# Image outputs of the last four heads computed on GpSimd, and their channels transposed once per pair

## The chip, the core and the metric

The kernel runs on one core of a Trainium2 chip. The core has five engines that work side by side, each through its own instructions in order: TensorE (PE in the profile, its weight loads PEld), VectorE (DVE), ScalarE (ACT), GpSimd (POOL) and SyncE (SP, which here only issues DMA transfers). They meet through semaphores. The metric is the device time of one execution in microseconds.

## What is computed

Two cross-attention layers run one behind the other over 64 batches of 256 tokens with 320 channels, in 20 heads of 16 channels. Each batch has 77 context rows of 512 numbers. Layer 0 is an attention over the 77 rows with a residual. Layer 1 splits its context into 73 text rows and 4 image rows, and the change lies in its image part:

```python
scores_t = jnp.einsum('bhsd,bhtd->bhst', q, k_t) * attn_scale
probs_t = jax.nn.softmax(scores_t, axis=-1)
text_out = jnp.einsum('bhst,bhtd->bhsd', probs_t, v_t)
...
attn_scores = jnp.einsum('bhsd,bhnd->bhsn', q, k_ip) * attn_scale
qsem = _l2norm(jnp.einsum('bhst,bte->bhse', probs_t, text_ehs))
sem = jnp.einsum('bhse,bne->bhsn', qsem, _l2norm(ip_ehs))
fused = attn_scores + SEM_SCALE * sem
probs_ip = jax.nn.softmax(fused, axis=-1) * spatial_mask[None, None, :, None]
ip_out = jnp.einsum('bhsn,bhnd->bhsd', probs_ip, v_ip)
...
out = (text_out + IP_SCALE * ip_out) @ W_out + b_out + residual
```

So for every token and head there are four image weights (`probs_ip`), and the image output is a weighted sum of four value rows.

## The kernel before

**Tiling.** All numbers are float32. Batches go in pairs `p` (32 of them), `b` is the batch within the pair. The 320 channels are held as two tiles of 128 (heads 0 to 15, "main") and one of 64 (heads 16 to 19, "last"). The last channels of both batches share one tile of 128 partitions: rows 0 to 63 are batch 0, rows 64 to 127 batch 1, and its 256 columns are tokens. `H` is 20, `HT` 16, `NIP` 4, `P` 128, `HALF` 64, `S` 256 tokens, in halves `s` of 128.

**Steps.** A unit is eight heads of 128 tokens, and a pair has ten. The main loop runs over steps `g`; step `k = g % 10` of pair `p = g // 10` does one unit of layer 0 and one of layer 1, which is 13 steps behind. Each step has a fixed body on TensorE: the semantic products of layer 1 (`semantics`, L755 and L761), the scores of both layers (`scores`, L641), then `transposed(1)` and `transposed(0)` (L705 and L706), which bring the softmax results into [key, token]. VectorE takes the maximum of the scores (L659), subtracts it (L661), and multiplies and sums (L772, L775, L687, L1136). ScalarE does the exponentials (L669, L672, L673) and the copies out of PSUM: L712 and L713 for `transposed(1)`, L731 and L732 (L720 and L723 for the last heads) for `transposed(0)`, and L1064 for the sums of the semantic products. L1064 frees the PSUM tile `sc` that the next step's L755 writes: there is one. GpSimd normalizes the weights of layer 0 (L692), whose result `transposed(0)` of the next step reads, and copies the image scores (`att`, L676).

**Fillers.** All other work is placed by hand into the steps by `fillers(k, p)`, in four lists: `begin` runs after the scores, `first` between `transposed(1)` and `transposed(0)`, `second` and `third` behind them, with the attention products of layer 0 (`attend`, L788 and L793, in the steps whose unit closes a block) between the two. TensorE, ScalarE, VectorE and GpSimd keep the order in which the program was written (`keep_order`); SyncE's transfers are ordered by the scheduler once the first steps are over.

**PSUM.** Eight banks: four for `sc`, two for the pool `pms` (matrix products) and two for the pool `ptr` (tag "tr", all transposes). Each call of `transposed` takes both buffers of `ptr`, first the one of L705, then the one of L706.

**The image path of a pair.** It runs two pairs behind, so `fillers` calls it with `p - 2`:

- `image_values` (steps 7 and 8, L475): per batch, 20 DMAs on SyncE, one per head, each bringing the batch's four image value rows from `vip_rows` in DRAM into the tile `vip` [80 rows (head, image row), 320 channels]; `place_image_values` (step 9, L480) masks it on GpSimd to a block diagonal.
- `text_output` (in the steps in which layer 1 finishes a batch: step 9 for batch 0, step 4 for batch 1): `by_head` (L850) divides the text sums into `an` [token, half, head, channel] on GpSimd. `text_transposed` (list `third` of steps 0 and 5) turns it into [channel, token]: per token half, two transposes for the main channels (L837) and one for the last channels (L838), into one `ptr` tile, and two copies by ScalarE (L840 main, L841 last).
- `image_scores`, `image_shifted`, `image_exponential`, `image_weights` make the four weights per token and head, in the steps after; `image_weights` writes the tile `iw` through `by_head`, in step 2 for batch 0 and step 7 for batch 1.
- `image_transposed` (step 7, list `second`): four transposes of `iw` (L914, K 128, 80 rows out) into one `ptr` tile and one ScalarE copy to `iwT` (L916).
- `image_attend` (step 8, list `begin`): the products of `vip` and `iwT` for the main channels (L926), copied by ScalarE (L936) and added to the text part by GpSimd (L938).
- `image_attend_last` (step 8, at the end of `second`): the products for the last channels (L947, two products of K 80, one per batch, side by side in the array; each is two instructions in the profile), added to the text part on VectorE (L951).
- `project` (begun in step 9, L528; its end at the start of the next step 0, L537) and `project_last` (L616) read the result.

**Neighbours of these on GpSimd.** `place_values(1, p - 1, 1)` in step 7 (L424 and L430 into `gv`, L438 and L444 into `gr`) reads the tiles `vm` and `v_rest` that SyncE fetches (L395); L755 reads `gv`, L761 reads `gr`, for batch 1 first in the next step 0. `place_gram` (L511, L515) and `keys_by_head` (L365, reading `kl`) are in step 8; `gram` (L499 to L502, and eight loads L506 into `g_rest`) in steps 0 and 6. SyncE also loads the context tile `ct` (L154), `cf` (L179) and `x` (L167, L169).

Of the kernel before, what the change touches and what calls it, by code (L numbers as in the profile page):

```python
# [8 lines left out]
F32 = mybir.dt.float32  # L9
# [54 lines left out]
def tile_two_cross_attentions(ctx: ExitStack, tc: tile.TileContext, a: dict, out: bass.AP):  # L64
# [179 lines left out]
    head_mask = blocks("head_mask", P, 8, D)  # L244
    for n in (4, 2):
        nc.gpsimd.tensor_add(head_mask[:, :n], head_mask[:, :n], head_mask[:, n : 2 * n])
    ip_mask = blocks("ip_mask", H * NIP, H, NIP)

# [218 lines left out]

    def image_values(p, b):  # L470

        n, r0 = H * NIP, (2 * p + b) * NIP
        vip = vips[p, b] = big.tile([n, C], F32, tag="vip", name=f"vip{p}_{b}", bufs=3)
        for h in range(H):
            nc.sync.dma_start(vip[h * NIP : (h + 1) * NIP, :], vip_rows[r0 : r0 + NIP, :])  # L475

    def place_image_values(p, b):
        n, vip = H * NIP, vips[p, b]
        v = vip.rearrange("p (h d) -> p h d", d=D)
        nc.gpsimd.tensor_tensor(v, v, ip_mask[:n].unsqueeze(2).broadcast_to([n, H, D]), ALU.mult)  # L480

    grams = {}

# [330 lines left out]
            nc.scalar.copy(last, ps[:, 1, :])  # L814


    def text_output(p, b):

        sums = stats[p, b][1]
        rec = small.tile([P, 2 * H], F32, tag="rec", name=f"rec{p}_{b}", bufs=2)  # L820
        nc.vector.reciprocal(rec, sums[:, :, NIP + D])
        an = big.tile([P, 2, H, D], F32, tag="an", name=f"an{p}_{b}", bufs=1)
        by_head(an, sums[:, :, NIP : NIP + D], rec)
        return an

    def text_transposed(p, b):

        an = made["an"]
        if b == 0:
            aTs[1, p] = channels("aT1", f"aT1_{p}", 1)  # L830
        main, last = aTs[1, p]
        rows = slice(b * HALF, (b + 1) * HALF)
        for s in range(2):
            ps = ptr.tile([P, 4, P], F32, tag="tr", name=f"atr{p}_{b}{s}")
            t = an[:, s].rearrange("p h d -> p (h d)")
            for i in range(2):
                nc.tensor.transpose(ps[:, i, :], t[:, i * P : (i + 1) * P], ident)  # L837
            nc.tensor.transpose(ps[: rows.stop, 2, :], t[:, C - rows.stop :], ident)  # L838
            t0 = b * S + s * P
            nc.scalar.copy(main[:, :, t0 : t0 + P], ps[:, :2])  # L840
            nc.scalar.copy(last[rows, s * P : (s + 1) * P], ps[rows, 2, :])  # L841

    one = const.tile([P, 1], F32, tag="one", name="one")

    def by_head(to, t, factor):

        n = t.shape[2]
        for s, h0, at in ((0, 0, 0), (1, HT, H), (1, 0, H + 4)):
            m = H if s == 0 else H - HT if h0 else HT
            nc.gpsimd.tensor_tensor(  # L850
                to[:, s, h0 : h0 + m], t[:, at : at + m],
                factor[:, at : at + m].unsqueeze(2).broadcast_to([P, m, n]), ALU.mult,
            )


    nums = {}
# [38 lines left out]
    def image_weights(p, b):  # L895

        num = nums[p, b]
        m = small.tile([P, 2, H], F32, tag="imx", name=f"imx{p}_{b}", bufs=1)
        r = m.rearrange("p s h -> p (s h)")
        nc.vector.tensor_reduce(r, num, AX.X, ALU.add)  # L900
        nc.vector.reciprocal(r, r)
        nc.gpsimd.tensor_mul(m, m, smask.unsqueeze(2).broadcast_to([P, 2, H]))
        to = weights[p, b] = small.tile([P, 2, H, NIP], F32, tag="iw", name=f"iw{p}_{b}", bufs=2)
        by_head(to, num, r)

    weights = {}

    def image_transposed(p):
        n = H * NIP
        ps = ptr.tile([P, 4, P], F32, tag="tr", name=f"itr{p}")  # L910
        for b in range(2):
            w = weights[p, b].rearrange("p s h t -> p s (h t)")
            for s in range(2):
                nc.tensor.transpose(ps[:n, 2 * b + s, :], w[:, s], ident)  # L914
        wT = big.tile([n, S2], F32, tag="iwT", name=f"iwT{p}", bufs=1)
        nc.scalar.copy(wT, ps[:n].rearrange("p j t -> p (j t)"))  # L916
        return wT
# [22 lines left out]
        t = big.tile([P, 2, S2], F32, tag="ip_out", name=f"ip_out{p}", bufs=1)  # L940
        return [lambda i=i: out_of(i) for i in range(2)]

    def image_attend_last(p):
        wT, last = made["wT"], aTs[1, p][1]
        ps = pms.tile([P, 512], F32, tag="ms", name=f"ipv{p}_2")
        for b in range(2):
            nc.tensor.matmul(  # L947
                ps[b * HALF : (b + 1) * HALF, :S], vips[p, b][:, 2 * P :], wT[:, b * S : (b + 1) * S],
                start=True, stop=True,
            )  # L950
        nc.vector.tensor_add(last, ps[:, :S], last)  # L951


    made = {}

    def fillers(k, p):
# [19 lines left out]
        elif k == 1:  # L976
# [3 lines left out]
                add(1, p, place_values, 0, p, 0)  # L980
            add(0, p, queries, 0, p, 2)
            add(1, p - 1, project, 0, p - 1)
            add(1, p - 1, place_gram, 0)
            add(1, p, keys_by_head, 0, p, 1)
            add(1, p - 1, keys_by_head, 1, p - 1, 0)
# [17 lines left out]
        elif k == 4:  # L1003
            if p == 0:
                add(0, p, image_keys, 1)
            else:
                add(0, p, keys, 1, p, 0)
            add(1, p - 1, values, 1, p - 1, 1)
            add(1, p + 1, first_queries, p + 1)
        elif k == 5:  # L1010
            if p == 0:
                add(0, p, image_keys, 2)
            add(0, p + 1, keys, 0, p + 1, 0)
            add(2, p - 2, text_transposed, p - 2, 1)
        elif k == 6:
            while len(made_rows) * P < min(NB, 2 * (p + 2)) * T:
                rows_todo.extend((len(made_rows), l) for l in range(2))
                made_rows.append(rows_todo[-1])
            for n in range(len(rows_todo) // 2):
                add(0, p, value_rows, *rows_todo.pop(0))  # L1020
            if p == 0:
                add(0, p, image_norms)
            else:
                add(1, p, keys, 1, p, 1)
            add(1, p - 1, gram, p - 1, 1)
            add(1, p, place_image_keys, p)
        elif k == 7:
            add(0, p + 1, keys, 0, p + 1, 1)
            add(1, p + 1, last_keys, p + 1)
            add(1, p - 2, lambda: made.update(wT=image_transposed(p - 2)))  # L1030
            add(1, p - 1, place_values, 1, p - 1, 1)
            add(1, p - 1, image_values, p - 1, 0)
            if p == 0:
                add(1, p, image_rows)
        elif k == 8:
            while rows_todo:
                add(0, p, value_rows, *rows_todo.pop(0))
            add(1, p - 1, place_gram, 1)
            add(1, p + 1, keys_by_head, 0, p + 1, 0)
            add(1, p - 1, image_values, p - 1, 1)  # L1040
            add(1, p - 2, image_attend_last, p - 2)
            add(3, p - 2, lambda: held.update(i=lambda: image_attend(p - 2)))
        else:
            add(0, p - 2, project, 1, p - 2)
            add(1, p + 1, values, 0, p + 1, 0)
            for b in range(2):
                add(1, p - 1, place_image_values, p - 1, b)
# [159 lines left out]
```

## Time and profile before

| what | value |
|---|---|
| median of 3 runs | 2614.46 us (2613.04 to 2614.5) |
| profiled execution, its own time | 2612.19 us |
| span of that profile | 2610.4 us |
| granted TensorE clock | 0.998 |
| L947 products, 128 instructions, busy together | 20.9 us |
| L838 transposes, 128 | 272 ns each in the records |
| L951 sums on VectorE, 32 | 415 ns each (median) |
| L841 copies on ScalarE, 128 | 262 ns each (median) |
| L480 masks on GpSimd, 64 | 727 ns each (median) |
| DMA share of the span, mean of 16 engines (SyncE's queue q1) | 18.0% |

In these rows a line is a line of the kernel, followed by the engine, the operation and the tiles (out<-in); "x" counts instructions. The records of TensorE overlap, since products are pipelined: a record of 0.27 us may cost 0.11 us when another follows. The chain of waits is better for that: it follows the end of the program back, and gives each piece only the time in which nothing else was the reason. An idle time in brackets stands before the instruction that ends it, with what released it. Times of day are in us from the start of the span; a pair takes 77.4 us in the steady part, or some more where a step has additional rows to project.

### The profile page before, as it was taken

Reading aid. Unit: us, or ns where it says so; the run is one execution under the profiler, and the core shown is the slowest. Engines: PE = TensorE matmul, PEld = TensorE weight load, DVE = VectorE, ACT = ScalarE, POOL = GpSimd, SP = SyncE. Lnnn points to the kernel's source line nnn. Section 1 sums busy time; section 2 is a strip of 40 time slices with the busy share of each in tenths; the row PEclk is TensorE's granted clock in tenths of the full one; section 3 lists DMA queues with packets and bytes.
Section 4 is the critical chain, followed back from the end, with each engine's and each line's share of the span. In section 5 each row is a group of like instructions: output and inputs, shape, how many; then the busy total and the mean of one; then the engine's idle time right before and its main releaser. Section 6 shows DMA issues by size and latency. Waiting matters only on the chain.

```text
span 2610.4 us, 74097 instructions
## 1 busy us (share of the span) xinstructions
PE 2552.0 (98%) x27026; PEld 1979.1 (76%) x27026; DVE 1971.3 (76%) x3641; ACT 1535.6 (59%) x3989; POOL 1439.9 (55%) x3514
## 2 busy tenths in 40 slices
PE   7999999999999999999999999999999999999998
PEld 5677777777777777777777777777777777777677
DVE  4577777777787777787777787777777778777864
ACT  3465665665665665665665665665665566666553
POOL 2456555566555556555556555556555565555542
PEclk9999999999999999999999999999999999999999
DMA  5212211112111112111112111112111112111100
GB/s 164 72 29 58 58 43 48 43 51 55 52 51 38 51 51 55 55 48 39 51 52 55 51 52 43 47 52 56 52 51 39 51 53 55 47 50 34 29 22 23
DMA packets 154658, 132.28 MB, mean 51 GB/s; under 512 B 48248, under 2 KB 132984, under 8 KB 154296
## 3 DMA queue, kind: packets, MB, share of 16 engines
q1 hardware_dynamic: 153432, 126.38, 18.0%
q8 instruction: 217, 3.56, 0.6%
q14 instruction: 145, 1.19, 0.2%
q10 hardware_dynamic: 864, 1.15, 0.1%
HBM read 89.53 MB, written 33.91 MB: 47 GB/s over the span
## 4 chain that ended last, share of the span: by engine, by line
PE 84%; DVE 7%; DMA 3%; ACT 2%; POOL 1%; issue 1%; SPq 1%; DVEq 0%; POOLq 0%; ACTq 0%
PE sc L755 12%; PE tr L705 11%; PE o_ps L528 8%; PE sc L641 7%; PE v_ps L379 6%; PE sc L761 4%; PE q_ps L528 4%; PE q_ps L555 4%; PE k_ps L334 3%; PE o_ps L616 3%; DVE w L661 3%; PE pv L788 2%; PE o_ps L537 2%; DVE mx L659 2%; PE q_ps L557 2%; PE rtr L706 2%
## 5 line engine op out<-in xcount | busy, mean ns | idle before, releaser
L659 DVE TENSOR_REDUCE mx<-sc 128x8 f32<-128x584 f32 (+1 forms) x640 | 497.3, 777 | 446.9 <-PE sc L641 446.8
L692 POOL TENSOR_TENSOR parts<-w,sm 128x512 f32<-128x512 f32 (+1 forms) x640 | 439.5, 707 | 301.9 <-ACT parts L673 177.8
L661 DVE TENSOR_TENSOR w<-sc,mx 128x616 f32<-128x616 f32 x640 | 511.8, 800 | 67.0 <-ACT w L669 0.5
L712 ACT COPY pt<-tr 128x512 f32<-128x512 f32 x320 | 186.8, 584 | 431.9 <-PE tr L705 427.5
L705 PE MATMUL tr<-ident,parts 128*128 128x128 f32 x2560 | 409.6, 283 | 12.5 <-POOL parts L692 5.2
L755 PEld LDWEIGHTS sc<-gv,pt 64*128 64x128 f32 x5120 | 316.9, 187 | 96.0 <-ACT sums L1064 47.3
L705 PEld LDWEIGHTS tr<-ident,parts 128*128 128x128 f32 x2560 | 282.5, 141 | 123.4 <-issue 88.0
L755 PE MATMUL sc<-gv,pt 64*128 64x94 f32 x5120 | 356.3, 278 | 17.4 <-ACT sums L1064 17.2
L676 POOL COPY att<-w 128x32 f32<-128x32 f32 x320 | 66.8, 209 | 469.7 <-DVE w L661 469.2
L669 ACT ACTIVATE w<-w 128x616 f32<-128x616 f32 x320 | 232.0, 725 | 96.7 <-DVE w L661 95.8
L687 DVE TENSOR_REDUCE sm<-w 128x8 f32<-128x616 f32 x320 | 247.9, 775 | 13.6 <-ACT w L669 13.6
L641 PE MATMUL sc<-kbd,q 32*128 32x154 f32 x5120 | 248.2, 306 | 1.0 <-ACT q L586 0.8
L528 PE MATMUL o_ps<-aT,wo 128*128 128x256 f32 x1024 | 231.6, 379 | 0.0
L1136 DVE TENSOR_REDUCE nrm<-prod 128x8 f32<-128x584 f32 x320 | 227.3, 710 | 0.4
L772 DVE TENSOR_TENSOR prod<-sc,parts 128x512 f32<-128x512 f32 x320 | 217.8, 681 | 4.0 <-PE sc L761 4.0
L528 PEld LDWEIGHTS o_ps<-aT,wo 128*128 128x128 f32 x1024 | 189.7, 190 | 23.0
L672 ACT ACTIVATE parts<-w 128x512 f32<-128x512 f32 x320 | 207.1, 647 | 0.0
L641 PEld LDWEIGHTS sc<-kbd,q 32*128 32x128 f32 x5120 | 187.0, 187 | 6.2 <-issue 5.4
L731 ACT COPY pt<-tr 128x512 f32<-128x512 f32 x256 | 151.1, 590 | 67.1 <-PE tr L705 66.8
L379 PE MATMUL v_ps<-wv,cf 128*128 128x320 f32 (+1 forms) x624 | 182.1, 438 | 0.0
L706 PE MATMUL rtr<-ident,parts 128*104 128x128 f32 (+1 forms) x640 | 174.8, 273 | 0.0
L1064 ACT COPY sums<-sc 128x168 f32<-128x168 f32 x320 | 96.4, 301 | 122.5 <-DVE prod L775 121.3
(151 smaller groups left out, 4840.0 us busy)
## 6 DMA issues: line engine op xcount, KB each, us to landing
vip<-vip_rows SPq DMA_DIRECT2D x1280, 5.0 KB
out_dram<-x SPq DMA_DIRECT2D x64, 256.0 KB
x<-in_x_dram SPq DMA_DIRECT2D x31, 512.0 KB
v_rows<-vs SPq DMA_DIRECT2D x38, 320.0 KB
vm<-v_rows SPq DMA_DIRECT2D x152, 80.0 KB
ct<-in_ctx_dram SPq DMA_DIRECT2D x32, 308.0 KB
cf<-in_ctx_dram SPq DMA_DIRECT2D x38, 256.0 KB
g_rest<-gram_rest SPq DMA_DIRECT2D x512, 0.5 KB
```

Source lines behind the costliest of these rows:

```text
L379: nc.tensor.matmul(ps[:n, :C], cfs[i][:, k, :n], wv[l][:, k, :], start=(k == 0), stop=(k == KE - 1))
L528: nc.tensor.matmul(ps[b][:, m, :], w[:, k, m * P : (m + 1) * P], main[:, k, b * S : (b + 1) * S], start=(k == 0 and m == 0), stop=False,)
L641: nc.tensor.matmul(ps[:, r, 2 * T * l : 2 * T * (l + 1)], q[rows, b, :] if part == 2 else q[rows, t0 : t0 + P], kbd[rows, part].rearrange( ...
L659: nc.vector.tensor_reduce(mx, sc[:, :, :, :nt], AX.X, ALU.max)
L661: nc.vector.tensor_tensor(w, sc, mx.unsqueeze(3).broadcast_to([P, 4, 2, T]), ALU.subtract)
L669: nc.scalar.activation(w, w, AF.Exp, scale=SCALE)
L687: nc.vector.tensor_reduce(sm, w, AX.X, ALU.add)
L692: nc.gpsimd.tensor_tensor(two[:, 8 * t0 : 8 * t1].rearrange("p (h t) -> p h t", h=8), w[:, :, t0:t1], sm.unsqueeze(2).broadcast_to([P, 8, ...
L705: nc.tensor.transpose(ps[:, i, :], flat[:, i * P : (i + 1) * P], ident)
L706: nc.tensor.transpose(pr[:n, 0, :], flat[:, 4 * P : 4 * P + n], ident)
L755: nc.tensor.matmul(ps[:, i % 2 * 2 + j, at : at + GV], pt[half_rows, i, :], gv[b][half_rows, part, i, :], start=start and i < 2, stop=False,)
L1136: nc.vector.tensor_reduce(eight(stats[q, b][2], u), prod, AX.X, ALU.add)
```

## The change

The four last heads leave the image path by TensorE. `iw`, `vip` and the mask shrink to 16 heads (64 rows, 256 channels, 16 DMAs per batch), and `image_attend_last` goes with its products and its sum. Instead:

- `by_head` writes the last heads (both token halves in one instruction) into a tile of their own: `lasts[p]` [token, half, batch, head, channel] for the text part, `iw_last` for the weights. It still has three instructions per call.
- `last_image_values` (steps 1 and 5) loads the batch's four value rows of 64 channels to all 128 partitions with one DMA that repeats its source (tile `vlast`, one buffer).
- `last_image_outputs` (steps 4 and 7) makes the image output as [token, head] on GpSimd: for each of the four image rows one product of [128, 2 x 4 x 16] (value row times weight) and one sum into `lasts[p]`.
- `last_transposed` (step 8, end of `second`) transposes `lasts[p]` for both batches at once: two transposes into one `ptr` tile, one ScalarE copy of 128x256 into the last channels.
- `text_transposed` keeps only the main channels.
- `place_values(1, p - 1, 1)` moves from step 7 to step 8, behind `keys_by_head`.

```diff
@@ -244,7 +244,7 @@
...
-    ip_mask = blocks("ip_mask", H * NIP, H, NIP)
+    ip_mask = blocks("ip_mask", HT * NIP, HT, NIP)
...
@@ -469,15 +469,22 @@
...
-        n, r0 = H * NIP, (2 * p + b) * NIP
-        vip = vips[p, b] = big.tile([n, C], F32, tag="vip", name=f"vip{p}_{b}", bufs=3)
-        for h in range(H):
-            nc.sync.dma_start(vip[h * NIP : (h + 1) * NIP, :], vip_rows[r0 : r0 + NIP, :])
+
+        n, r0 = HT * NIP, (2 * p + b) * NIP
+        vip = vips[p, b] = big.tile([n, 2 * P], F32, tag="vip", name=f"vip{p}_{b}", bufs=3)
+        for h in range(HT):
+            nc.sync.dma_start(vip[h * NIP : (h + 1) * NIP, :], vip_rows[r0 : r0 + NIP, : 2 * P])
 
     def place_image_values(p, b):
-        n, vip = H * NIP, vips[p, b]
+        n, vip = HT * NIP, vips[p, b]
         v = vip.rearrange("p (h d) -> p h d", d=D)
-        nc.gpsimd.tensor_tensor(v, v, ip_mask[:n].unsqueeze(2).broadcast_to([n, H, D]), ALU.mult)
+        nc.gpsimd.tensor_tensor(v, v, ip_mask[:n].unsqueeze(2).broadcast_to([n, HT, D]), ALU.mult)
+
+    def last_image_values(p, b):
+
+        r0 = (2 * p + b) * NIP
+        v = vips[p, b, "last"] = small.tile([P, NIP, HALF], F32, tag="vlast", name=f"vlast{p}_{b}", bufs=1)
+        nc.sync.dma_start(v, vip_rows[r0 : r0 + NIP, 2 * P :].unsqueeze(0).broadcast_to([P, NIP, HALF]))
...
@@ -814,13 +821,17 @@
...
+    lasts = {}
+
     def text_output(p, b):
 
         sums = stats[p, b][1]
         rec = small.tile([P, 2 * H], F32, tag="rec", name=f"rec{p}_{b}", bufs=2)
         nc.vector.reciprocal(rec, sums[:, :, NIP + D])
-        an = big.tile([P, 2, H, D], F32, tag="an", name=f"an{p}_{b}", bufs=1)
-        by_head(an, sums[:, :, NIP : NIP + D], rec)
+        an = big.tile([P, 2, HT, D], F32, tag="an", name=f"an{p}_{b}", bufs=1)
+        if b == 0:
+            lasts[p] = big.tile([P, 2, 2, H - HT, D], F32, tag="an_last", name=f"an_last{p}", bufs=1)
+        by_head(an, lasts[p][:, :, b], sums[:, :, NIP : NIP + D], rec)
         return an
...
@@ -828,29 +839,48 @@
...
-        main, last = aTs[1, p]
-        rows = slice(b * HALF, (b + 1) * HALF)
+        main = aTs[1, p][0]
         for s in range(2):
             ps = ptr.tile([P, 4, P], F32, tag="tr", name=f"atr{p}_{b}{s}")
             t = an[:, s].rearrange("p h d -> p (h d)")
             for i in range(2):
                 nc.tensor.transpose(ps[:, i, :], t[:, i * P : (i + 1) * P], ident)
-            nc.tensor.transpose(ps[: rows.stop, 2, :], t[:, C - rows.stop :], ident)
             t0 = b * S + s * P
             nc.scalar.copy(main[:, :, t0 : t0 + P], ps[:, :2])
-            nc.scalar.copy(last[rows, s * P : (s + 1) * P], ps[rows, 2, :])
+
+    def last_image_outputs(p, b):
+
+        v = vips[p, b, "last"].rearrange("p t (h d) -> p t h d", d=D)
+        w, to = weights[p, b, "last"], lasts[p][:, :, b]
+        part = [P, 2, H - HT, D]
+        for t in range(NIP):
+            prod = small.tile(part, F32, tag="ip_last", name=f"ip_last{p}_{b}{t}", bufs=1)
+            nc.gpsimd.tensor_tensor(
+                prod, v[:, t].unsqueeze(1).broadcast_to(part), w[:, :, :, t].unsqueeze(3).broadcast_to(part), ALU.mult
+            )
+            nc.gpsimd.tensor_add(to, to, prod)
+
+    def last_transposed(p):
+
+        ps = ptr.tile([P, 4, P], F32, tag="tr", name=f"ltr{p}")
+        for s in range(2):
+            nc.tensor.transpose(ps[:, s, :], lasts[p][:, s].rearrange("p b h d -> p (b h d)"), ident)
+        nc.scalar.copy(aTs[1, p][1], ps[:, :2].rearrange("p s t -> p (s t)"))
...
-    def by_head(to, t, factor):
+    def by_head(to, last, t, factor):
 
         n = t.shape[2]
-        for s, h0, at in ((0, 0, 0), (1, HT, H), (1, 0, H + 4)):
-            m = H if s == 0 else H - HT if h0 else HT
-            nc.gpsimd.tensor_tensor(
-                to[:, s, h0 : h0 + m], t[:, at : at + m],
-                factor[:, at : at + m].unsqueeze(2).broadcast_to([P, m, n]), ALU.mult,
-            )
+        for out, at in ((to[:, 0], 0), (last, HT), (to[:, 1], H + 4)):
+            m = H - HT if out is last else HT
+            full = [P, 2, m, n] if out is last else [P, m, n]
+            k = 2 * m if out is last else m
+            x, f = t[:, at : at + k], factor[:, at : at + k]
+            if out is last:
+                x = x.rearrange("p (s h) d -> p s h d", s=2)
+                f = f.rearrange("p (s h) -> p s h", s=2)
+            nc.gpsimd.tensor_tensor(out, x, f.unsqueeze(len(full) - 1).broadcast_to(full), ALU.mult)
...
@@ -900,13 +930,16 @@
...
-        to = weights[p, b] = small.tile([P, 2, H, NIP], F32, tag="iw", name=f"iw{p}_{b}", bufs=2)
-        by_head(to, num, r)
+        to = weights[p, b] = small.tile([P, 2, HT, NIP], F32, tag="iw", name=f"iw{p}_{b}", bufs=2)
+        last = weights[p, b, "last"] = small.tile(
+            [P, 2, H - HT, NIP], F32, tag="iw_last", name=f"iw_last{p}_{b}", bufs=1
+        )
+        by_head(to, last, num, r)
...
-        n = H * NIP
+        n = HT * NIP
...
-    def image_attend_last(p):
-        wT, last = made["wT"], aTs[1, p][1]
-        ps = pms.tile([P, 512], F32, tag="ms", name=f"ipv{p}_2")
-        for b in range(2):
-            nc.tensor.matmul(
-                ps[b * HALF : (b + 1) * HALF, :S], vips[p, b][:, 2 * P :], wT[:, b * S : (b + 1) * S],
-                start=True, stop=True,
-            )
-        nc.vector.tensor_add(last, ps[:, :S], last)
...
@@ -980,6 +1003,7 @@
...
+            add(1, p - 2, last_image_values, p - 2, 0)
...
@@ -1006,12 +1030,14 @@
...
+            add(1, p - 2, last_image_outputs, p - 2, 0)
             add(1, p + 1, first_queries, p + 1)
         elif k == 5:
...
             add(2, p - 2, text_transposed, p - 2, 1)
+            add(1, p - 2, last_image_values, p - 2, 1)
...
@@ -1028,7 +1054,7 @@
...
             add(1, p - 2, lambda: made.update(wT=image_transposed(p - 2)))
-            add(1, p - 1, place_values, 1, p - 1, 1)
+            add(1, p - 2, last_image_outputs, p - 2, 1)
             add(1, p - 1, image_values, p - 1, 0)
...
@@ -1038,7 +1064,8 @@
...
             add(1, p - 1, place_gram, 1)
             add(1, p + 1, keys_by_head, 0, p + 1, 0)
             add(1, p - 1, image_values, p - 1, 1)
-            add(1, p - 2, image_attend_last, p - 2)
+            add(1, p - 1, place_values, 1, p - 1, 1)
+            add(1, p - 2, last_transposed, p - 2)
             add(3, p - 2, lambda: held.update(i=lambda: image_attend(p - 2)))
```

## The prediction

> **What bounds the kernel now.** I read four views. First the busy shares and the chain of waits on the page. Then the chain and the timeline in order of time over one pair of batches (1244.9 to 1322.3 us). Then the waits of TensorE, VectorE and SyncE, and last the groups of GpSimd kept apart by shape. Between those two times TensorE is busy 77.02 of 77.40 us, GpSimd 44.88, ScalarE 47.55, VectorE 61.12, and the next pair takes the same 77.40 us. So TensorE's own sequence, its waits included, is the period, and all else matters only where TensorE would wait for it.
>
> ```profile
> PE 2552.0 (98%) x27026; PEld 1979.1 (76%) x27026; DVE 1971.3 (76%) x3641; ACT 1535.6 (59%) x3989; POOL 1439.9 (55%) x3514
> PE 84%; DVE 7%; DMA 3%; ACT 2%; POOL 1%; issue 1%; SPq 1%; DVEq 0%; POOLq 0%; ACTq 0%
> ```
>
> Three places of the pair are touched on TensorE. **Step 8**, where the products of `image_attend_last` (L947) stand between the transposes and the next step's L755 (timeline: start, duration, engine):
>
> ```profile
> 1313.71 0.27 PE L706 MATMUL rtr<-ident,parts 128*104 128x128 f32 x1
> 1313.80 0.30 ACT L1064 COPY sums<-sc 128x168 f32<-128x168 f32 x1
> ...
> 1313.92 0.65 PE L947 MATMUL ipv<-iwT,vip 80*64 80x256 f32 x4
> 1313.99 0.61 ACT L731 COPY pt<-tr 128x512 f32<-128x512 f32 x1
> ...
> 1314.50 1.13 PE L755 MATMUL sc<-gv,pt 64*128 64x94 f32 x16
> ```
>
> L947 starts at 1313.92 and L755 at 1314.50: it costs 0.58. While it runs, ScalarE is still copying the PSUM tile of `transposed(0)` out (L731, ends 1314.60). **Step 0** and **step 5** hold the text transposes (chain in order of time):
>
> ```profile
> 1252.59 0.11 PE atr L838
> 1252.70 0.22 PE atr L837 x2
> 1252.92 0.11 PE atr L838
> 1253.03 1.06 PE sc L755 x16
> ```
>
> ```profile
> 1292.97 0.15 DVE prod L775
> 1293.13 0.02 issue
> 1293.15 0.31 ACT sums L1064
> 1293.46 0.04 issue
> 1293.50 1.13 PE sc L755 x16
> ```
>
> In step 0 the chain is all TensorE; each L838 is 0.11. At the end of step 5 it is not: L755 waits for VectorE and then ScalarE (its wait is 0.32), whatever TensorE finished before.
>
> **The change, part by part, per pair.**
>
> (1) Step 0: two L838 go, 2 x 0.11 = 0.22 (by start times, 1252.43 to 1252.54 and 1252.76 to 1252.96, up to 0.28). TensorE sets the end there: -0.22, at most -0.28.
>
> (2) Step 5: two L838 go, and TensorE only waits 0.22 longer for L1064: 0. The chain behind that wait starts at VectorE's L659 in the same step, which the change leaves alone. Were that cover gone it would be -0.22.
>
> (3) `itr` loads 64 columns of weights for 80: its four loads are 0.115 to 0.123, L838's with 64 columns 0.11. That is -0.02 for the four.
>
> (4) Step 8: L947 goes, and two transposes into a new PSUM tile come. The pool has two buffers; `transposed(0)` has just taken both, so the new tile takes the first of them, which L731 frees at 1314.60. Before, nothing on TensorE needed that here. In step 7 `itr` waits for the very same copy: L731 ends at 1305.79 and L914 starts at 1305.84, 0.05 later, and its four transposes take 0.57 until 1306.41. So the first new transpose starts at 1314.65. Two of them take 2 x 0.11 = 0.22 at the least; by L914, whose first one after a wait costs more (0.57 - 3 x 0.11 = 0.24), 0.35. L755 then starts between 1314.87 and 1315.00, against 1314.50: +0.37 to +0.50. I take +0.45, nearer to L914, the row that also starts after a wait. Queued behind the wait are L755, L641 and all of step 9, and VectorE waits for L641 (it was idle 1.15 before L659 in that step), so nothing absorbs it. This holds in 27 of the 32 places, where L731 ends 0.67 to 0.69 after L947 starts; two more have 0.87 and 0.58, one waits otherwise, two are the drain. I count 30.
>
> (5) VectorE loses L951 (0.415), in front of that idle 1.15: 0. ScalarE loses four L841 (0.26 each) and gains one 128x256 copy (0.39, as L840) behind L673, with 1.82 of idle before its next copy: 0.
>
> (6) GpSimd gains, per batch, four products and four sums of 128x128 elements; no row has that shape:
>
> ```profile
> L464 POOL TENSOR_TENSOR vr<-vr,rest 104x128 f32<-104x128 f32 x64 | 25.6, 400 | 0.0
> ...
> L884 POOL TENSOR_TENSOR num<-num,att 128x160 f32<-128x160 f32 x64 | 33.5, 523 | 5.0
> ```
>
> A product is like L464, 0.40; a sum without broadcast lies between L365's 0.44 for 154 elements and L884's 0.52 for 160, so 0.46 as a middle. An instruction that needs the one in front starts 0.07 after it (L883 ends 1252.30, L884 starts 1252.37); independent ones overlap by 0.04. So 4 x (0.40 + 0.46) + 8 x 0.07 = 4.0 us; bounds 8 x 0.36 = 2.9 and 8 x (0.52 + 0.07) = 4.7. The places for it:
>
> ```profile
> 1287.19 1.58 POOL L850 TENSOR_TENSOR an<-sums,rec 128x320 f32<-128x320 f32 x3
> 1292.44 0.21 POOL L676 COPY att<-w 128x32 f32<-128x32 f32 x1 [3.68 <-DVE w L661]
> ```
>
> ```profile
> 1318.29 0.44 POOL L365 TENSOR_TENSOR kbd<-kl,head_mask 128x154 f32<-128x154 f32 x1
> ...
> 1322.25 0.27 POOL L866 TENSOR_TENSOR least<-sums 128x40 f32<-128x40 f32 x1 [3.52 <-ACT sums L1064]
> ```
>
> The bracket is GpSimd's idle time before the line. Batch 0 runs in the 3.68 of step 4; what sticks out (0.3, at most 1.0) delays L676 and meets the 0.85 idle before L883. Batch 1 takes the place of `place_values` in step 7, which was 3.56 long (1309.08 to 1312.64), so L938 and L692 come 0.44 later (-0.7 to +1.1); L692 would end at 1316.9 and its transposes start at 1320.37. `place_values` now runs in the 3.52 of idle and ends at 1322.7 (1323.4 at worst). Its first half feeds L755 (ready about 1320.6, wanted 1322.3), its second L761, wanted at 1323.38 plus the 0.45 of (4). Hidden by about 1 us; without that cover each us late is a us of TensorE.
>
> [...]
>
> (7) `by_head` stays at three instructions, and `vip`'s mask (0.73 to about 0.62) shrinks: 0.
>
> (8) SyncE issues 8 fewer `vip` loads per pair (7.28 / 20 = 0.36 each, -2.9) and two `vlast` loads (cf's 0.41 to x's 1.15 each). The second may start only when GpSimd has done batch 0 (about 1292.8), in a stretch in which SyncE waits anyway for a `ct` buffer until 1300.55, and is wanted at 1309.1. The reload of `vm` moves from 1311.29 to about 1320.6 behind `place_values`; its reader L453 comes at 1331.6. Queued behind such waits are `g_rest`, `kl` and `vr`. Hidden: 0.
>
> Sum per pair: -0.22 - 0.02 + 0.45 = +0.21; times 30, **+6.3 us**; bounds 30 x (0.37 - 0.30) = +2 and 30 x (0.50 - 0.22) = +8. The drain (2593 to 2599) trades L947 and L951 for 4 us of GpSimd beside `itr`, L926 and L934: 0, give or take 1. The profiled execution was 2612.19 (span 2610.4), within 0.1% of the median 2614.46; the median gives 2614.5 + 6.3 = **2621 us**.
>
> **Rivals.**
>
> A, the forecast: TensorE waits at the new tile, 2616 to 2624.
>
> B, faster: the transposes find their buffer free. Then step 8 costs two transposes inside the wait for L1064 (ends 1314.10), L755 starts at about 1314.16, -0.34, with -0.24 from (1) and (3): -0.58 x 30 = -17 us, 2597. It decides if L731 ends before 1313.9. Against it: L731 follows L380 and L1064 on ScalarE, none of which changes. For it: TensorE's plain work does shrink, by 0.44 + 0.58 - 0.22 = 0.80 per pair, 24 us.
>
> C, much slower: GpSimd comes late. If SyncE puts the second `vlast` behind `gram` and `g_rest` (1302.6 to 1309.6), it lands at perhaps 1312 and the eight instructions end at 1316.2: the transposes wait 1.55 longer and L761 0.6 for `gr`; +2.4 per pair, +72 us, 2686. Half that lateness gives some 2650. Against it: SyncE's order follows readiness (`ct` is issued 0.03 after its buffer frees), and `vlast` is ready earlier than `gram`.
>
> D, no change: waits that I count fully are partly covered, within 5 us of 2614.5.
>
> **How the numbers follow.** About 0.2%, 5.2 us, is what a measurement of this kernel can tell from no change. A 0.64, B 0.13, C 0.13, D 0.10. A's values lie around that bound; I give 0.45 of its 0.64 to slower and 0.19 to the same. Slower: 0.45 + 0.13 = 0.58; same 0.19 + 0.10 = 0.29; faster 0.13. Predicted 2621. The range 2609 to 2635 holds A, D and the mildest part of C and leaves out B and most of C; A alone would be 2616 to 2624.
>
> **What would show it.** Right: the page after has no L947 and no L838; the new transposes show a wait of 0.6 to 0.7 on L731, some 30 times; L755 behind them starts 0.4 to 0.5 later after L706; the pair's period grows from 77.40 to about 77.6; GpSimd's busy time rises by about 64 x 4 us less overlaps, to some 1650 to 1690, without new waits of TensorE on it. Wrong: no such wait (B), or waits of L761, L755 or the new transposes on GpSimd, or of GpSimd on `vlast`, `vm` or `vip` (C).

## The result, and the profile after

The changed kernel took 2639.7 us in the median of 4 runs (2636.1 to 2642.27), the kernel before 2614.3 beside it (2613.04 to 2614.5): a ratio of 1.0097, 95% interval 1.008 to 1.0115. It is slower by 25.4 us; 6.3 were forecast. The profiled execution took 2639.39 with a span of 2637.7, 27.3 above the span before.

The page, busy times and the chain that ended last, after:

```profile
PE 2539.4 (96%) x26834; PEld 1972.5 (75%) x26834; DVE 1958.0 (74%) x3609; ACT 1513.5 (57%) x3893; POOL 1649.2 (63%) x4026
PE 69%; DVE 12%; POOL 7%; ACT 4%; DMA 3%; issue 2%; SPq 2%; DVEq 0%; POOLq 0%; ACTq 0%
```

TensorE has less to do (2552.0 to 2539.4) and yet the span grew: the chain runs less over TensorE (84% to 69%), more over VectorE (7% to 12%) and GpSimd (1% to 7%). The new work is in TensorE's waits (engine, line, what it waited for; us in total, times, longest):

```profile
PE ltr L867 <- ACT pt L738: 23.6, 30, 1.6
PE sc L762 <- ACT sums L1091: 20.3, 32, 2.3
PE tr L712 <- ACT pt L719: 15.3, 34, 2.3
...
PE itr L947 <- POOL iw L883: 3.5, 2, 3.3
```

The first line is the wait that was forecast, 30 times. The second is old (L755 on L1064, 17.2 in 35). The third was 4.0 us in 5 waits before, and the fourth wasn't there: neither was forecast.

**Step 8**, timeline after (start, duration, engine):

```profile
1321.80 0.27 PE L713 MATMUL rtr<-ident,parts 128*104 128x128 f32 x1
1321.88 0.30 ACT L1091 COPY sums<-sc 128x168 f32<-128x168 f32 x1
1322.07 0.60 ACT L738 COPY pt<-tr 128x512 f32<-128x512 f32 x1
...
1322.82 0.41 PE L867 MATMUL ltr<-ident,an_last 128*128 128x128 f32 x2 [0.75 <-ACT pt L738]
1323.16 1.13 PE L762 MATMUL sc<-gv,pt 64*128 64x94 f32 x16
```

From L713 to the next semantics it is 1.36 us, 0.79 before: +0.57. The copy ends at 1322.67, `ltr` starts 0.15 later and holds TensorE for 0.34.

**Step 1**, first before and then after. GpSimd's `place_values(0)` (L464 is its last instruction), the subtraction of the largest image score behind it, ScalarE's exponential, the copy of layer 1's tile queued behind that, and TensorE's next transposes:

```profile
1332.88 0.40 POOL L464 TENSOR_TENSOR vr<-vr,rest 104x128 f32<-104x128 f32 x1
...
1333.24 0.46 POOL L890 TENSOR_TENSOR num<-num,most 128x160 f32<-128x160 f32 x1
1333.73 0.34 ACT L893 ACTIVATE num<-num 128x160 f32<-128x160 f32 x1 [2.48 <-POOL num L890]
1333.98 0.57 ACT L712 COPY pt<-tr 128x512 f32<-128x512 f32 x1
...
1334.69 0.63 PE L705 MATMUL tr<-ident,parts 128*128 128x128 f32 x4
```

```profile
1341.57 0.40 POOL L464 TENSOR_TENSOR vr<-vr,rest 104x128 f32<-104x128 f32 x1
...
1341.93 0.47 POOL L920 TENSOR_TENSOR num<-num,most 128x160 f32<-128x160 f32 x1
1342.43 0.34 ACT L923 ACTIVATE num<-num 128x160 f32<-128x160 f32 x1 [2.82 <-POOL num L920]
...
1342.68 0.57 ACT L719 COPY pt<-tr 128x512 f32<-128x512 f32 x1
...
1343.39 0.63 PE L712 MATMUL tr<-ident,parts 128*128 128x128 f32 x4 [0.31 <-ACT pt L719]
```

Step 0's semantics began at 1322.31 before and at 1330.98 after. Counted from there, the subtraction starts at 10.93 before and 10.95 after, and the transposes at 12.38 and 12.41. This chain goes round by VectorE, ScalarE and GpSimd and has a length of its own. TensorE finishes step 0 in 7.86 us where it took 8.08, and then stands for the difference in step 1.

**The tail.** The image weights of the very last batch, after:

```profile
2609.81 0.63 POOL L883 TENSOR_TENSOR an<-sums,rec 128x256 f32<-128x256 f32 x1
2610.40 0.41 POOL L858 TENSOR_TENSOR ip_last<-vlast,iw_last 128x128 f32<-128x128 f32 x1
...
2613.98 0.45 POOL L861 TENSOR_TENSOR an_last<-an_last,ip_last 128x128 f32<-128x128 f32 x1
2614.39 0.49 POOL L913 TENSOR_TENSOR num<-sums,nrm 128x160 f32<-128x160 f32 x1
...
2618.30 0.30 PE L947 MATMUL itr<-ident,iw 128*64 128x128 f32 x1 [3.31 <-POOL iw L883]
```

Batch 0's eight instructions stand in GpSimd's queue in front of the image scores of batch 1 (L913), for 4.0 us, and nothing is left behind which they could hide. Before, the transposes of these weights follow without a wait:

```profile
2593.10 1.06 PE L914 MATMUL itr<-ident,iw 128*80 128x128 f32 x4
```

From the start of the last semantics (2604.82; before 2583.05) to the end of the span it takes 32.9 us instead of 27.4.

**Where the 27.3 us lie.** A pair is counted from the start of step 8's semantics to the next such start. +0.8 stand before the first of these; +14.7 in the 28 pairs that follow; +6.3 in the 26 steps after them, in which layer 0 ends (the drain); +5.5 in the tail. A regular pair is 0.62 longer; 28 of them would be 17.4, and 2.7 come back in single pairs, 1.8 of it in steps 4 that waited longer before (in one 9.91 against 8.90).

### The profile page after: what moved, and what is told of

Read it like the earlier page. It is cut to its first block, busy times and chain, and to the rows that moved or that the text cites. A ratio compares the mean times of both kernels' runs of the same rounds, so it can differ in the third digit from the quotient of the medians.

```text
span 2637.7 us, 73764 instructions
## 1 busy us (share of the span) xinstructions
PE 2539.4 (96%) x26834; PEld 1972.5 (75%) x26834; DVE 1958.0 (74%) x3609; ACT 1513.5 (57%) x3893; POOL 1649.2 (63%) x4026
## 4 chain that ended last, share of the span: by engine, by line
PE 69%; DVE 12%; POOL 7%; ACT 4%; DMA 3%; issue 2%; SPq 2%; DVEq 0%; POOLq 0%; ACTq 0%
PE sc L762 10%; PE tr L712 9%; PE o_ps L535 8%; PE v_ps L379 6%; PE sc L648 5%; PE q_ps L562 4%; PE q_ps L535 4%; DVE w L668 4%; PE sc L768 4%; PE k_ps L334 3%; DVE mx L666 3%; PE q_ps L564 2%; PE o_ps L623 2%; PE rtr L713 2%; DVE prod L779 2%
## 5 line engine op out<-in xcount | busy, mean ns | idle before, releaser
L762 PEld LDWEIGHTS sc<-gv,pt 64*128 64x128 f32 x5120 | 318.5, 188 | 94.0 <-ACT sums L1091 41.6
L762 PE MATMUL sc<-gv,pt 64*128 64x94 f32 x5120 | 358.1, 279 | 22.9 <-ACT sums L1091 20.3
L713 PE MATMUL rtr<-ident,parts 128*104 128x128 f32 (+1 forms) x640 | 174.9, 273 | 0.0
L334 PE MATMUL k_ps<-ct,wk 128*128 128x146 f32 (+1 forms) x1024 | 155.0, 294 | 8.1 <-DMA ct<-in_ctx_dram 8.1
```

What stands on the lines that cost most here:

```text
L334: nc.tensor.matmul(pv, wk[l][:, k, i * P : (i + 1) * P], cts[p][:, k, :, :nt], start=(k == 0), stop=(k == KE - 1))
L762: nc.tensor.matmul(ps[:, i % 2 * 2 + j, at : at + GV], pt[half_rows, i, :], gv[b][half_rows, part, i, :], start=start and i < 2, stop=False,)
```

## The experiments

One table first, read from the timelines of the profiled runs. "Pair" is the difference of a regular pair to the kernel before, "drain" that of the 26 steps in which layer 0 ends, "tail" the time from the last semantics to the end. Steps in us. Each row is one profiled run, and the granted clock in the drain differs between them, from 1.00 throughout (before, e5, e10) down to 0.50 in a window of 10 us (e9; see the part on the drain). Each ratio below is to the kernel before, run in the same session; its medians there lie between 2613.46 and 2616.16.

| kernel | step 8 | step 0 | step 1 | pair | drain | tail | median |
|---|---|---|---|---|---|---|---|
| before | 7.09 | 8.08 | 9.40 | 0 | 0 | 27.4 | 2614.3 |
| after | 7.67 | 7.86 | 9.65 | +0.62 | +6.3 | 32.9 | 2639.7 |
| e1_ltr_pms | 6.75 | 8.01 | 10.19 | +0.40 | +1.9 | 32.2 | 2626.09 |
| e2_place0_step1 | 7.67 | 7.85 | 9.29 | +0.26 | +5.2 | 32.7 | 2627.42 |
| e3_no_products | 7.61 | 7.85 | 9.66 | +0.57 | +6.0 | 26.9 | 2708.58 |
| e4_before_place8 | 7.09 | 8.07 | 9.45 | +0.06 | +2.5 | 27.4 | 2624.65 |
| e5_all_three | 6.75 | 8.03 | 9.29 | -0.49 | -0.6 | 27.3 | 2596.49 |
| e6_after_tail | 7.67 | 7.86 | 9.66 | +0.62 | +8.9 | 27.3 | 2632.42 |
| e7_pms_place0 | 6.75 | 8.02 | 9.29 | -0.51 | +0.9 | 32.2 | 2602.96 |
| e8_before_place0 | 7.09 | 8.08 | 9.29 | -0.11 | +1.8 | 27.5 | 2612.44 |
| e9_fill_wait | 7.67 | 7.85 | 9.65 | +0.62 | +11.1 | 33.4 | 2640.49 |
| e10_fill_drain | 7.67 | 7.86 | 9.64 | +0.62 | +1.5 | 32.8 | 2634.2 |

### The buffer of the new transposes (e1_ltr_pms)

```diff
-        ps = ptr.tile([P, 4, P], F32, tag="tr", name=f"ltr{p}")
+        ps = pms.tile([P, 4, P], F32, tag="ms", name=f"ltr{p}")
```

> The changed kernel with the tile of the two new transposes taken from the pool of matrix products (pms) in place of the pool of transposes. Buffer theory (the wait is for the copy of transposed(0) that holds the tile): the wait of ltr on ScalarE's pt copy is gone, step 8 falls from 7.67 to about 6.75 us (the next step's semantic products then start behind the sums' copy), but GpSimd has only 0.31 us of idle time left before its next square, so step 1 grows by some 0.6 through the chain image maximum, image exponential, pt copy: about -0.3 us per pair, 2628 to 2633 us. Rival (ltr is late because GpSimd's sums into an_last are late): the wait stays, now on GpSimd, step 8 stays at 7.67, 2640.

2626.09 us (2623.77 to 2631.01), ratio 1.0043 (1.0027 to 1.0059), below the 2628 to 2633 expected. With a free buffer the wait is gone and step 8 is 0.34 shorter than before, which is what rival B of the prediction gave for it. But step 1 grows to 10.19, and TensorE's wait for the copy of layer 1's tile nearly doubles:

```profile
PE tr L712 <- ACT pt L719: 28.3, 35, 2.3
```

So the buffer costs 0.92 in step 8 (7.67 less 6.75). In a regular pair 0.70 of it are given back in steps 0 and 1; where step 8 carries extra value rows, nothing is, and the pair is 0.30 shorter than before.

### The chain of step 1 (e2_place0_step1)

```diff
         if k == 0:
-            if p:
-                add(2, p, place_values, 0, p, 0)
...
         elif k == 1:
...
             if p == 0:
...
-                add(1, p, place_values, 0, p, 0)
+            add(1, p, place_values, 0, p, 0)
```

> The changed kernel with place_values(0, p, 0) moved from step 0 to the second list of step 1, so that GpSimd reaches the shifted image scores 1.7 us earlier. Chain theory (the 0.22 us that step 0 gains make TensorE wait in step 1 for the pt copy, which stands behind the image exponential on ScalarE, which waits for GpSimd): step 1 falls from 9.65 back to 9.40, step 0 stays at 7.85, -0.25 us per pair, 2630 to 2634 us. Rival (step 1 is longer for another reason, the moved place_values(1) or the copy of 128x256): step 1 stays at 9.65, 2640.

2627.42 us (2626.55 to 2628.62), ratio 1.0046 (1.0031 to 1.0061), again below what was expected. With GpSimd's three instructions behind the subtraction instead of in front of it, step 1 takes 9.29, 0.36 less than in the changed kernel and 0.11 less than before (only 9.40, the length before, was expected). Steps 8 and 0 stay as they were. The wait in question:

```profile
PE tr L712 <- ACT pt L719: 2.6, 4, 0.7
```

### GpSimd's products (e3_no_products)

```diff
-        for t in range(NIP):
+        for t in range(0):
```

(with the two instructions of the loop taken out: the image outputs of the last four heads are left out.)

> The changed kernel without the four products and four sums per batch on GpSimd: the image outputs of the last four heads are left out. Theory (in the steady part the eight instructions are hidden, and they cost only in the drain, where the steps are short): the ten steps of a steady pair keep their lengths (7.67, 7.82, 7.85, 9.65, ...), the drain from the last pairs on is 7 to 9 us shorter, 2629 to 2634 us. Rival (GpSimd's 4 us per batch are what costs): steps 8 and 1 fall back to 7.1 and 9.4, 2605 to 2616.

2708.58 us (2707.09 to 2713.64), ratio 1.0361 (1.0343 to 1.0379): the expected 2629 to 2634 can't be tested by the whole time, since the first four pairs are 80 us longer (10.3, 28.3, 31.3 and 10.6), with waits for loads that neither kernel has. The pairs in the middle can: +0.57, against +0.62 with the products. So the eight instructions per batch cost at most 0.05 a pair there. The drain stays long without them, +6.0, and the tail is 26.9: it is the tail that they cost.

### The moved `place_values(1)` alone (e4_before_place8)

The kernel before, with that one line moved from step 7 to step 8:

```diff
         elif k == 7:
-            add(1, p - 1, place_values, 1, p - 1, 1)
         elif k == 8:
+            add(1, p - 1, place_values, 1, p - 1, 1)
```

> The kernel before with one thing of the change alone: place_values(1, p - 1, 1) moved from step 7 to the end of step 8. Theory (the move is hidden): steps as before, 2612 to 2617 us. Rival (the move makes GpSimd late in steps 9 to 1): step 1 or the semantic products of step 0 wait on GpSimd, 0.2 us per pair or more, 2620 or above.

2624.65 us (2622.39 to 2627.14), ratio 1.0035 (1.0022 to 1.0048), more than the 2612 to 2617 expected. It lies in the rival's range, but not for the rival's reason: step 0 is the same and step 1 only 0.05 longer. Regular pairs pay 0.06. But five pairs pay in step 4 (14.32 against 9.91 in the worst, 8.0 us in all), where GpSimd waits for the reloads of `vm` and `v_rest`, and TensorE behind it:

```profile
PE q_ps L528 <- ACT kT L337: 8.0, 5, 3.9
```

Before, that wait was 1.6 us in 3. In the changed kernel it isn't there: step 4 takes 8.68 to 9.05 in those five pairs. The changed kernel has eight `vip` loads a pair fewer on SyncE (and two `vlast` loads more); that these make the difference is an explanation, not a finding, and it wasn't tried. No run shows that the drain's +2.5 is a cost of the move: the granted clock fell there (0.70 in 2470 to 2480 us).

### All that was found at once (e5_all_three), and its parts (e6, e7, e8)

The edits of e1 and e2, and for the last pair alone the eight instructions of batch 0 one step earlier:

```diff
         elif k == 3:
+            if p - 2 == NP - 1:
+                add(1, p - 2, last_image_outputs, p - 2, 0)
         elif k == 4:
-            add(1, p - 2, last_image_outputs, p - 2, 0)
+            if p - 2 < NP - 1:
+                add(1, p - 2, last_image_outputs, p - 2, 0)
```

> The changed kernel with three edits: ltr's tile from the pool of the products (tag ms), place_values(0) of the current pair in step 1 instead of step 0, and the eight GpSimd products of batch 0 of the last pair alone issued one step earlier (step 3, not step 4). My theory now: the extra 25 us are three things, (a) step 8's wait for the buffer, +0.58 a pair, which without it is -0.34, (b) step 0's -0.22, which is given back in step 1 (+0.26) because GpSimd's place_values(0) stands in front of num minus most; with it behind, step 1 is -0.10, (c) the drain: about +5 in the steps after the last full pair and +5.5 behind the last weighted sums, where batch 1's image weights queue behind batch 0's eight products. Expected against before: step 8 -0.34, step 0 -0.22, step 1 -0.10, -0.66 a pair, -19 over the pairs; the tail from the last semantics to the end from 32.9 to 28 to 29 us (before 27.4); drain steps still +3 to +5. Total 2597 to 2605 us. Rival (what is won is always given back by the next chain of the pair): 2609 to 2618.

2596.49 us (2595.93 to 2601.66), ratio 0.9936 (0.9924 to 0.9948): faster than both kernels. Step 8 is -0.34 and step 1 -0.11, as expected; the tail, 27.3, is below the 28 to 29 expected; step 0 gives -0.05 in most pairs and -0.22 only in those whose step 8 carries extra value rows, and the drain costs nothing where +3 to +5 were expected (the granted clock stays at 1.00 there in this profiled run). Step 8 in it:

```profile
1313.00 0.59 ACT L738 COPY pt<-tr 128x512 f32<-128x512 f32 x1 [2.04 <-PE tr L712]
1313.00 1.14 PE L544 MATMUL o_ps<-aT,wo 64*128 64x256 f32 x8
...
1314.10 1.13 PE L762 MATMUL sc<-gv,pt 64*128 64x94 f32 x16
```

TensorE now multiplies (L544) while ScalarE copies, and semantics follows without a wait for the copy.

The tail alone, e6_after_tail:

> The changed kernel with only the eight products of batch 0 of the last pair one step earlier. My theory: the wait of 3.3 us for the last image weights is gone, the tail from the last semantics to the end falls from 32.9 to 28 to 30 us, steady steps as in the changed kernel: 2633 to 2637 us. Rival (the tail is long because of the lower granted clock, not because of the products): the tail stays within 1 us of 32.9, 2638 to 2640 us.

2632.42 us (2631.52 to 2638.03), ratio 1.0074 (1.006 to 1.0089). The tail is 27.3, below the 28 expected at least, so all 5.5 us come from the queue on GpSimd. The same place in it:

```profile
2613.99 0.63 POOL L883 TENSOR_TENSOR an<-sums,rec 128x256 f32<-128x256 f32 x1
2615.44 0.50 POOL L913 TENSOR_TENSOR num<-sums,nrm 128x160 f32<-128x160 f32 x1 [0.82 <-DVE nrm L912]
...
2619.36 0.30 PE L947 MATMUL itr<-ident,iw 128*64 128x128 f32 x1 [0.19 <-POOL iw L883]
```

L913 follows the text outputs with 0.82 of waiting for its own input, and TensorE's wait falls from 3.31 to 0.19, which is 3.1 of the 5.5 us. The other 2.4 lie behind it: from this transpose to the end of the span it takes 19.38 us in the changed kernel and 16.95 here. These 10 us behind it, first in the changed kernel and then in e6, show why (busy time of PE, PEld, DVE, ACT and POOL with counts; granted clock; DMA share; GB/s):

```profile
2618.00:2628.00 10.00, 9.55 (x41) 7.90 (x42) 1.29 (x2) 0.95 (x2) 4.12 (x11) 0.66 0.01 2
```

```profile
2619.00:2629.00 10.00, 9.34 (x56) 7.18 (x56) 1.29 (x2) 0.95 (x2) 4.19 (x11) 1.00 0.01 2
```

So the wait costs twice, 3.1 us as itself and 2.4 as a slower TensorE behind it (a granted clock of 0.66 for 1.00). All twelve profiled runs agree: the six with the wait of 3.3 us (after, e1, e2, e7, e9, e10) have a mean clock of 0.51 to 0.66 in the 10 us behind it, the six without (before, e3, e4, e5, e6, e8) have 1.00. (The drain of this profiled run was longer than the changed kernel's, +8.9; see below.)

The two edits without the tail, e7_pms_place0:

> The changed kernel with ltr's tile from the pool of the products and place_values(0) in step 1, the tail as it was. My theory: -0.66 a pair against before as in the run with all three edits, the tail 32 to 33 us: 2601 to 2610 us, 4 to 5 us above the run with all three. Rival (the two edits don't add up, one chain limits both): step 1 +0.3 to +0.8 over before, 2618 to 2626 us.

2602.96 us (2601.84 to 2607.46), ratio 0.9966 (0.9953 to 0.9979). They add up: e1's 10.19 in step 1 is 9.29 here, so what e1 ran into was the same chain. (The pair is -0.51 where -0.66 was expected, since step 0 gives little here too.)

The kernel before with e2's edit, e8_before_place0:

> The kernel before with only place_values(0) of the current pair in step 1 instead of step 0. It tells whether what the last runs win is the change's or that move's alone. My theory: in the kernel before the transposes of layer 1 in step 1 wait for the buffer by at most 0.1 us, so the move takes at most 0.10 a pair from step 1 and leaves every other step: 2611 to 2615 us. Rival (the move is the gain): below 2608 us. Another way: GpSimd's other work in step 1 comes later and lengthens later steps, as the move of place_values(1) to step 8 did: 2616 to 2625 us.

2612.44 us (2609.77 to 2617.34), ratio 0.9992 (0.9983 to 1.0002). Regular pairs gain 0.11 and nothing more. So the gain of e5 is the change's own, once its three costs are taken off; and the 0.11 says that the chain already set the end of step 1 in the kernel before, by a hair.

### The drain (e9_fill_wait, e10_fill_drain)

In the steps in which layer 0 ends, the profile after shows a lower granted clock. Windows of 10 us as above, before and after, at the same steps:

```profile
2460.00:2470.00 10.00, 6.40 (x92) 4.92 (x92) 9.48 (x19) 8.54 (x22) 4.91 (x11) 1.00 0.01 2
2470.00:2480.00 10.00, 7.45 (x100) 6.22 (x100) 8.57 (x16) 5.95 (x19) 4.75 (x15) 1.00 0.02 4
2480.00:2490.00 10.00, 8.37 (x106) 5.89 (x107) 8.51 (x16) 6.47 (x18) 7.10 (x19) 1.00 0.12 27
```

```profile
2480.00:2490.00 10.00, 6.15 (x85) 4.44 (x78) 8.68 (x16) 6.62 (x19) 8.03 (x18) 1.00 0.06 13
2490.00:2500.00 10.00, 8.33 (x87) 7.02 (x89) 7.42 (x15) 5.11 (x16) 3.55 (x13) 0.83 0.02 4
2500.00:2510.00 10.00, 7.64 (x88) 5.74 (x80) 6.64 (x12) 5.83 (x16) 8.57 (x15) 0.88 0.08 18
2510.00:2520.00 10.00, 10.00 (x80) 8.38 (x79) 6.21 (x13) 3.69 (x9) 5.45 (x20) 0.78 0.16 35
```

At a granted clock of 1.00 the 16 products of L762 take 1.13 us; at 2508.01, behind a wait of `ltr` of 1.65, they take 2.03. First the fill at that wait alone:

```diff
+        if p == NP - 3:
+            fill = pms.tile([P, 4, P], F32, tag="ms", name="fill")
+            for i in range(14):
+                nc.tensor.transpose(fill[:, i % 4, :], ident, ident)
         ps = ptr.tile([P, 4, P], F32, tag="tr", name=f"ltr{p}")
```

> The changed kernel with 14 transposes of the identity, into a buffer of the products' pool, in front of ltr of the third last pair only: TensorE is busy during its wait of 1.65 us for the buffer in the step that comes out of the drain. In the changed kernel that wait is followed by semantics of 2.03 instead of 1.13 us and a step 9 of 10.82 instead of 7.81 us. My theory: the granted clock falls because TensorE stood still, so the fill leaves step 8 at 7.7 to 7.9 us and brings step 9 back to 7.8 to 8.2: -2.6 to -3.0 us, 2636 to 2637.5 us, and semantics there takes 1.13 us. Rival (the slow stretch has another cause, such as the transfers of the drain or the power drawn by all engines): semantics stays near 2.0 us and step 9 at 10.4 to 10.9 us, 2639 to 2640 us.

2640.49 us (2635.3 to 2643.22), ratio 1.0093 (1.0077 to 1.011), not the 2636 to 2637.5 expected. Step 9 behind the fill is 7.81 as expected, but the slow stretches lay in front of it, and step 8 there took 10.59:

```profile
2480.00:2490.00 10.00, 9.45 (x73) 6.64 (x72) 6.21 (x12) 4.55 (x14) 6.59 (x15) 0.50 0.06 13
2490.00:2500.00 10.00, 7.90 (x75) 6.73 (x73) 8.21 (x15) 5.59 (x16) 3.30 (x12) 0.79 0.02 4
2500.00:2510.00 10.00, 9.27 (x75) 6.64 (x76) 6.32 (x12) 4.17 (x12) 6.08 (x12) 0.55 0.08 17
```

So the loss isn't that one wait's. Then all five waits over 0.9 us of steps 4 to 8, with the same transposes (`fill(n, name)` writes `n` of them into a buffer of `pms`):

```diff
+        if g == NP * NU - 5:
+            fill(18, "fill4")
...
+        if p == NP - 1 and k in (5, 6):
+            fill(12 if k == 5 else 18, f"fill{k}")
...
+        if p == NP - 3:
+            fill(7, "fill7")
...
+        if p == NP - 3:
+            fill(14, "fill8")
```

> The changed kernel with transposes of the identity (7 to 18 of them, 0.125 us each) in front of each of the five waits of TensorE over 0.9 us in steps 4 to 8 of the last pair of layer 0, into a buffer of the products' pool. With the fill at one wait alone the slow stretch lay elsewhere in the drain and the time stayed. My theory: the granted clock falls because TensorE is idle for about a quarter of these 40 us, so with all gaps filled it stays at 1.00, semantics takes 1.13 us throughout, the drain's +2.1 in step 6 and +3.0 in step 9 go, and 3 to 5 us are gained: 2634 to 2637 us. Rival (the clock falls in the drain for another reason than TensorE's gaps): windows of granted clock under 0.9 remain, 2638 to 2643 us.

2634.2 us (2633.1 to 2635.86), ratio 1.007 (1.0053 to 1.0087; it overlaps that of the changed kernel by a little, the two sets of runs don't: 2635.86 at most against 2636.1 at least). The clock in the same steps:

```profile
2480.00:2490.00 10.00, 9.42 (x110) 7.80 (x109) 8.75 (x17) 6.54 (x20) 6.95 (x16) 1.00 0.06 15
2490.00:2500.00 10.00, 9.09 (x132) 7.24 (x131) 7.84 (x15) 5.00 (x16) 5.35 (x16) 1.00 0.02 4
2500.00:2510.00 10.00, 9.17 (x87) 7.72 (x86) 7.59 (x13) 5.72 (x14) 9.34 (x21) 1.00 0.10 21
```

It stays at 1.00, and the drain costs 1.5 instead of 6.3. So some 4.8 us of the drain are the clock in the profiled run of the changed kernel. That it falls because TensorE stands still there is what this speaks for, but one profiled run with all waits filled doesn't show it: of the eleven profiled runs without these five fills nine have a lowered clock in the drain, and two, before and e5, have none, with the waits unfilled. Among the nine are e4 and e8, the kernel before with one move (0.70 and 0.75 in a window of 10 us), and their drains cost 2.5 and 1.8. So part of the +6.3 may be that the profiled run of the kernel before happened to have no such stretch; neither that nor how large a part was measured. Behind which wait it falls stays open: in e5 a wait of 2.3 us in step 6 is there and the clock was not seen to fall, in e1 the same wait is followed by a semantics of 2.03.

## Why the prediction was right in direction and wrong in size

**Right.** (4)'s mechanism, the copy that holds the buffer: 30 waits, and e1 takes them away. (6) in the pairs: a product 0.41, a sum 0.46, eight instructions 4.0 us, hidden (e3: 0.05 a pair at most); GpSimd's busy time 1649 where 1650 to 1690 was named. (2), (5), (7) and (8): steps 2 to 7 of a regular pair are the same within 0.01. B's -0.34 for step 8, to the hundredth, in e1. Rival C's queue on `vlast` did not come.

**Wrong, by size.** (4) measured +0.58 a pair for +0.45, outside its bound of 0.50: `ltr` starts 0.15 after the copy's end, not 0.05, and the two transposes hold TensorE for 0.34, where +0.45 has 0.30. The trace has a semaphore instruction of 51 ns in TensorE's queue of weight loads at `ltr`, none such was counted; what the other 0.05 of the start is was not measured. Over 28 pairs, 3.6 us.

**Wrong, by reasoning.** (1) took step 0's -0.22 as net, because the chain of waits there is all TensorE. It didn't ask what is next when TensorE is early. The chain from the same step's semantics over GpSimd's `place_values(0)` to the transposes of step 1 had no slack: -0.22 came, and +0.25 came back (e2 and e8 show the owner). Over 28 pairs 7.0 us.

**Wrong, the two ends.** The "0, give or take 1" of the prediction is for 2593 to 2599 us, which lies in the tail; there it was +5.5 (e6): 3.1 of waiting and 2.4 of a lower granted clock behind the wait. I named the lines beside which GpSimd's 4 us would run, but not the ones behind it in GpSimd's own queue: rival C was right in kind there, GpSimd comes late, in a place where I hadn't put it. The steps in which layer 0 ends had no term of their own; they measured +6.3, of which some 4.8 are granted clock (e10 against the changed kernel) and part may be chance in the profiled runs.

Together: 28 times 0.62 for 28 times 0.21, +11.5; drain and tail +11.4 above the 0.4 that the forecast's other two pairs come to; the start +0.8; less 2.7 in single pairs. That is the 21.0 us by which the span's +27.3 misses the forecast +6.3. The range, 2609 to 2635, was too narrow for it: without the 11.8 at the ends the measured 25.4 would have stayed inside. It had bounds for each term in the steady pair and hardly any for the two ends.

## What to carry to other kernels

When a step gets shorter on the engine that sets its end, follow the other chain that starts with the same step and ends in the next, and measure its slack before the saving is booked; here it was nothing, and one move of an unrelated instruction freed it. The transposes into a pool whose buffers were just taken waited for the copy-out in front of them (0.75 us here, in 30 places up to 1.6), so look for a pool that is free at that place. And price the last pair by itself: batch 0's 4.0 us of GpSimd, hidden in every regular pair, stood bare in the queue there, and a wait of 3.3 us of TensorE cost another 2.4 behind it.

## What the hardware showed unexpectedly

The forecast had no term for the granted clock. In the changed kernel's drain, where no wait of TensorE is above 2.32 us, it falls: with five waits of 0.96 to 2.32 us in 32 us it is down to 0.78 in a window of 10 us, and 16 products take 2.03 us for 1.13, 1.8 times as long. In e9 it fell to 0.50 behind the first of them, of 2.26 us; the kernel before has the same wait at the same place and stayed at 1.00 in its profiled run, but with one move (e8) it fell right behind that wait (0.75). In e5 it isn't seen to fall in the drain at all, nor in e10 with the waits filled (1.00, one profiled run). In the tail, behind the wait of 3.3 us, it fell in six runs of six (0.51 to 0.66 in the 10 us behind it). What makes it fall in the drain was not shown.

The times spread with it: the kernel before ran from 2611.49 at a mean granted clock of 0.999 to 2621.59 at 0.994, ten us apart, without any change to it.
